# Adding P1 into a PSUM bank in a Strassen product of a graph attention kernel

## The chip, the cores and the metric

The kernel runs on one core of one Trainium2 chip. The metric is the device time of one execution in microseconds (us). Before the change it is 2387.96 us, the median of three runs (2386.17 to 2392.22). The engines are TensorE (PE in the profile; PEld is its weight load), VectorE (DVE), ScalarE (ACT), GpSimd (POOL) and SyncE (SP), which issues most of the loads. TensorE writes its results into PSUM[...]; the other memory on the core is SBUF.

## The reference

All data are fp32. The input x is 128 graphs of 64 nodes with 512 features; one adjacency matrix serves all of them.

```python
h = jnp.maximum(_layernorm(x, axis=-1), 0.0)
x = x + _L0_gnn_ref(h, adj, W_heads, ...)

def _gat_heads(x, adj, W, a):
    Wh = jnp.einsum('bnf,hfo->bhno', x, W)
    f1 = jnp.einsum('bhno,ho->bhn', Wh, a[:, :O])
    f2 = jnp.einsum('bhno,ho->bhn', Wh, a[:, O:])
    e = f1[:, :, :, None] + f2[:, :, None, :]
    e = jnp.where(e > 0, e, LEAKY_ALPHA * e)
    e = jnp.where(adj[None, None] > 0, e, NEG_INF)
    attn = jax.nn.softmax(e, axis=-1)
    return jnp.einsum('bhnm,bhmo->bhno', attn, Wh)
...
h = jax.nn.elu(_gat_heads(enc_inputs, adj, W_heads, a_heads))
h = jnp.transpose(h, (0, 2, 1, 3)).reshape(B, N, -1)
out = _gat_heads(h, adj, W_out[None], a_out[None])[:, 0]
out = jax.nn.elu(out)
ffn = jnp.maximum(out @ w1 + b1, 0.0) @ w2 + b2
y = ffn + out
...
return (y - mu) / jnp.sqrt(var + LN_EPS) * ln_gamma + ln_beta
```

There are four heads of 512 x 512 (W_heads), an output layer of 2048 x 512 (W_out) and a feed-forward of two 512 x 512 matrices (w1, w2).

## The kernel before

The 8192 rows are cut into 64 tiles of 128 rows, and four tiles make a group; 16 groups (0 to 15) are worked off one after the other. All large products are done as Strassen products in Winograd's form: a 512 x 512 by 512 x 512 product is cut into quadrants, seven products P1 to P7 of half the size are made, and the four quadrants of the result are sums of them:

- C11 = P1 + P2
- C12 = P1 + P6 + P5 + P3
- C21 = P1 + P6 + P7 + P4
- C22 = P1 + P6 + P7 + P5

The sums that the right-hand sides need are made beforehand: for the weights once, at the start (`weight_sums`, L199), and for the data in each unit (`sums`, L328).

One such product is a *unit* (`unit`, L257). A unit owns three PSUM banks: bank 1 collects P1 and P2, bank 5 collects P5 and P3, bank 6 collects P6, P7 and P4, all by TensorE's own accumulation. What the accumulation can't share between banks is done by the function `after(p)` (L263), which is called behind the last matmul of each product: it copies P1 to SBUF (s1, by ScalarE), adds t = P6 + P1 and s15 = P5 + P1 (VectorE, PSUM to SBUF), and hands each quadrant to the unit's `post`, as one bank and at most one SBUF tile to be added to it. A product may begin in a bank only when all earlier readers of that bank are done: P2 waits for the copy s1, P7 for t, P3 for s15, P4 for the addition of C22.

Four kinds of unit exist, told apart in the profile by the letter in the names (g_a is a bank of unit a, t_a its tile t):

- a (`project1`, L557): one head of one group, so 64 of them. Its `post` runs elu on each quadrant: two ScalarE operations (L541, L542) and one on VectorE (L543). C21 is then also added to C22 by GpSimd (L580), as a sum for unit b.
- b (`project2`, L599): the output layer of one group, with P1 to P7 each in four parts, one for each head. Its `post` writes the quadrants to wh, and some of its products release GpSimd to make the next sums (L610).
- c and d (`feed_forward`, L685): the two feed-forward products. `post1` of c adds the bias and takes the maximum with zero on ScalarE (L722); `post2` of d adds each part of a quadrant to the output tile o as soon as it is there, on VectorE for those straight from PSUM and on GpSimd for the tiles s1, t and s15 (L733).

The order of the products is written out: in unit a 1, 6, 5, 2, 7, 3, 4, where the late P4 of a head is put behind P1 and P6 of the next head (`late`, L593). Between two parts of a unit, small steps of other stages are strung in (`run`, L248): during the four heads of group g the scores, softmax and second attention of group g-1 (`stage_e`), and during unit b of group g the attention of group g+1, the units c and d of group g-1, the final normalisation of group g-1 (`finish`, L735) and the start of group g+2 (`stage_a`).

Each engine works off its instructions in one fixed order. That order comes from the program with priorities: what `after` issues is drawn 150 places forward (`tc.high_priority(AHEAD)`, L289). An instruction that waits holds up all behind it on its engine. The PSUM pool has six banks that go round among the units and the attention (`bank`, L78) and two for small things (`aux`).

Of the kernel before, what the change touches and what calls it, by code (L numbers as in the profile page):

```python
# [11 lines left out]
ALU = mybir.AluOpType  # L12
# [10 lines left out]
def gat_preln_kernel(  # L23
# [28 lines left out]
    nc = tc.nc  # L52
# [25 lines left out]
    def bank(name):  # L78
        return ps.tile([P, 2, T], FP, tag="mm", name=name)
# [164 lines left out]
    def flush_late():  # L244
        while late:
            late.pop(0)()
# [10 lines left out]
    def unit(name, product, post, order):  # L257


        own = {1: 1, 2: 1, 5: 5, 3: 5, 6: 6, 7: 6, 4: 6}  # L260
        gb, sb = {}, {}

        def after(p):  # L263
            if p in (1, 5, 6):
                nm = {1: "s1", 5: "s15", 6: "t"}[p]
                sb[nm] = wk.tile([P, 2, T], FP, tag=nm, name=f"{nm}_{name}")
                if p == 1:
                    nc.scalar.copy(sb[nm], gb[1])  # L268
                else:
                    nc.vector.tensor_tensor(sb[nm], gb[p], sb["s1"], ALU.add)  # L270
                post(nm, sb[nm])
            elif p == 2:
                post("c11", gb[1], None)
            elif p == 7:
                post("c22", gb[6], sb["s15"])
            elif p == 3:
                post("c12", gb[5], sb["t"])
            else:
                post("c21", gb[6], sb["s1"])

        def part(p, i, n):
            def fn():
                if i == 0:
                    subs[p] = product(p)
                    if p == own[p]:
                        gb[p] = bank(f"g{p}_{name}")
                subs[p][i](gb[own[p]], p == own[p] and i == 0)
                if i == n - 1:
                    with tc.high_priority(AHEAD):  # L289
                        after(p)  # L290
            return fn

        subs = {}
        n = product(None)
        return [part(p, i, n) for p in order for i in range(n)]
# [242 lines left out]
    def elu(dst, src, name):  # L538

        ex = wk.tile([P, 512], FP, tag="elu", name=f"ex{name}", bufs=3)  # L540
        nc.scalar.activation(ex, src, AF.Relu, scale=-1.0)  # L541
        nc.scalar.activation(ex, ex, AF.Exp, scale=-1.0)  # L542
        nc.vector.scalar_tensor_tensor(dst, ex, -1.0, src, ALU.add, ALU.max)  # L543

    def flat(ap):
        return ap.rearrange("p a b -> p (a b)")

    def quadrant(what):
        return int(what[1]) - 1, int(what[2]) - 1
# [7 lines left out]
    def project1(g, h):  # L557


        z = ZB[g]  # L560
        first = (g, h) == (0, 0)
        if h == 0:
            for b in ("11", "12", "S1", "22"):
                tag = "hS" if b == "S1" else "h" + b
                H1[b] = big.tile([P, H, 2, T], FP, tag=tag, name=f"h{b}_{g}")
        sums = {6: 0, 7: 1, 3: 2}
        blk = {1: "11", 2: "12", 4: "22", 5: "S1"}

        def post(what, a, b=None):
            if what[0] != "c":  # L570
                return
            nm = {"c11": "11", "c12": "12", "c21": "S1", "c22": "22"}[what]
            dst = H1[nm][:, h]
            if b is None:
                elu(flat(dst), flat(a), f"{what}_{g}_{h}")
            else:
                nc.vector.tensor_tensor(dst, a, b, ALU.add)  # L577
                elu(flat(dst), flat(dst), f"{what}_{g}_{h}")
            if what == "c21":
                nc.gpsimd.tensor_tensor(dst, dst, H1["22"][:, h], ALU.add)  # L580

        s = unit(
            f"a{g}_{h}", product_t(h, lambda p: ZSUM[h][sums[p]] if p in sums else z[blk[p]][:, h]),
            post, (1, 2, 6, 5, 7, 3, 4) if first else (1, 6, 5, 2, 7, 3, 4),
        )

        def next_sums():
            if h + 1 < H:
                z_sums(g, h + 1)

        return [
            s[0], lambda: (s[1](), flush_late()), lambda: (s[2](), next_sums()), s[3], s[4],
            lambda: (s[5](), late.append(s[6])),  # L593
        ]
# [4 lines left out]
    def project2(g):  # L599
        slot = {1: "11", 2: "12", 3: "12", 4: "22", 5: "S1", 6: "11", 7: "S1"}  # L600
        h1 = dict(H1)
        wh = big.tile([P, G, FO], FP, tag="wh2", name=f"wh2_{g}")
        WH2[g] = wh

        def post(what, a, b=None):
            behind = {"s1": ("11", "S1", "11"), "s15": ("S1", "22", "11"), "c11": ("12", "12", "11")}
            if what in behind:
                dst, x0, x1 = (h1[n] for n in behind[what])
                for h in range(H):
                    nc.gpsimd.tensor_tensor(dst[:, h], x0[:, h], x1[:, h], ALU.subtract)  # L610
            if what[0] != "c":
                return
            r, c = quadrant(what)
            dst = wh[:, 2 * r:2 * r + 2, c * Q:(c + 1) * Q]
            if b is None:
                nc.scalar.copy(dst, a)
            else:
                nc.vector.tensor_tensor(dst, a, b, ALU.add)

        ms = [H + h for h in range(H)]  # L620
        return unit(
            f"b{g}", product_n(ms, lambda p, i: h1[slot[p]][:, i]), post, (1, 5, 6, 2, 7, 3, 4)
        )
# [61 lines left out]
    def feed_forward(g):  # L685

        o = OUT[g]
        OT, RT = [], []

        def transpose_out(j):  # L690
            if j % 2 == 0:
                OT.append(big.tile([P, KC, T], FP, tag=f"ot{j // 2}", name=f"ot{j // 2}_{g}"))
            pt = aux([P, KC, P], f"pto{g}_{j}")
            for k in range(KC):
                nc.tensor.transpose(pt[:, k, :], o[:, j, ts(k, P)], ident)  # L695
            nc.scalar.copy(OT[j // 2][:, :, ts(j % 2, P)], pt)
            nc.gpsimd.tensor_tensor(o[:, j], o[:, j], b2s, ALU.add)
            if j == G - 1:
                bl[1] = blocks(OT, f"o{g}")

        def blocks(tt, name):
            s2, s3, s4 = new_sums(name)
            a11, a12 = tt[0][:, 0:2], tt[0][:, 2:4]
            s1, a22 = tt[1][:, 0:2], tt[1][:, 2:4]
            nc.vector.tensor_tensor(s1, s1, a22, ALU.add)
            sums(nc.vector, s1, a11, a12, a22, s2, s3, s4)
            return {1: a11, 2: a12, 3: s4, 4: a22, 5: s1, 6: s2, 7: s3}

        bl = {}

        def post1(what, a, b=None):
            if what[0] != "c":
                return
            if not RT:
                RT.extend(big.tile([P, KC, T], FP, tag=f"rt{i}", name=f"rt{i}_{g}") for i in range(2))
            r, c = quadrant(what)
            dst = RT[r][:, 2 * c:2 * c + 2]
            if b is not None:
                nc.vector.tensor_tensor(dst, a, b, ALU.add)
                a = dst  # L720
            for k in range(2):
                nc.scalar.activation(  # L722
                    dst[:, k], a[:, k], AF.Relu, bias=b1s[:, 2 * c + k:2 * c + k + 1]
                )
            if what == "c21":
                bl[2] = blocks(RT, f"r{g}")

        def post2(what, a, b=None):

            r, c = {"t": (0, 1), "s15": (1, 1), "s1": (1, 0)}.get(what) or quadrant(what)  # L730
            dst = o[:, 2 * r:2 * r + 2, c * Q:(c + 1) * Q]
            eng = nc.vector if what[0] == "c" else nc.gpsimd
            eng.tensor_tensor(dst, a, dst, ALU.add)  # L733

        def finish(j):  # L735
            t = G * g + j
            xr = load(t, "xr")
            nc.gpsimd.tensor_tensor(xr, xr, bs, ALU.add)
            y = o[:, j]
            mean, rstd = norm_stats(y, "n2", t)  # L740
            nc.vector.scalar_tensor_tensor(y, y, mean, gs, ALU.subtract, ALU.mult)
            nc.vector.scalar_tensor_tensor(y, y, rstd, xr, ALU.mult, ALU.add)
            nc.sync.dma_start(out=of[ts(t, P), :], in_=y)

        f1 = unit(f"c{g}", product_t(M1, lambda p: bl[1][p]), post1, (1, 2, 6, 5, 7, 3, 4))
        f2 = unit(f"d{g}", product_n([M2], lambda p, i: bl[2][p]), post2, (1, 6, 5, 2, 3, 7, 4))
        return (
            [lambda j=j: transpose_out(j) for j in range(G)], f1 + f2,
            [lambda j=j: finish(j) for j in range(G)],
        )  # L750
# [125 lines left out]
```

## Time and profile before

| what | us |
|---|---|
| time, median of 3 runs | 2387.96 |
| profiled span | 2389.7 |
| TensorE busy | 2324.9 |
| VectorE busy | 1455.6 |
| GpSimd busy | 1064.1 |
| ScalarE busy | 780.7 |
| one group in the steady part (1641.4 to 1784.9) | 143.5 |
| the same for the second and third group | 146.5 |

The operations that the change touches, with the mean duration of one:

| operation | engine and line | count | ns |
|---|---|---|---|
| copy of P1 to SBUF (s_a) | ACT L268 | 64 | 575 |
| t = P6 + P1 (t_a) | DVE L270 | 64 | 685 |
| s15 = P5 + P1 (s_a) | DVE L270 | 64 | 683 |
| C21 of unit a | DVE L577 | 64 | 687 |
| last step of elu, source in PSUM (C11) | DVE L543 | 64 | 682 |
| the same, source in SBUF (C12, C22) | DVE L543 | 128 | 794 |
| the same, source in SBUF (C21) | DVE L543 | 64 | 953 |
| copy of a quadrant of unit b | ACT L616 | 16 | 586 |

Lines of the profile are read like this: the start, the duration, the engine, the line of the program, the operation, and "out<-in" by the names of the tiles. A bracket at the end tells how long the engine stood idle ahead of it and what ended that. A matmul of 128x256 takes about 380 ns from its start to its end, but in a row they start every 0.216 us, so one product of a unit (eight such rows) takes 1.73 us of TensorE. A profile numbers a wait by the instruction that waited and the one that released it; "issue" stands for time in which nothing that the profile shows was awaited.

### The profile page before, as it was taken

What the parts mean: (1) busy time and instruction counts of PE and PEld (TensorE: products, weight loads), DVE (VectorE), ACT (ScalarE), POOL (GpSimd) and SP (SyncE); (2) the same over time, 40 slices, a digit from 0 to 9 for tenths busy, and PEclk for the clock granted to TensorE, in tenths of its full rate; (3) what the DMA queues carried; (4) which work ended last, traced back from release to release, by engine and by line L of the source; (5) the groups of instructions that cost most, each with busy time, mean ns of one, the idle gap of its engine ahead of it and who ended that gap; (6) DMA issues with size and microseconds to landing.
All of it is one profiled execution on the core that took longest, in us unless ns stands there. A gap on an engine that the chain in (4) does not pass through costs nothing.

```text
span 2389.7 us, 32881 instructions
## 1 busy us (share of the span) xinstructions
PE 2324.9 (97%) x11805; PEld 1943.2 (81%) x11805; DVE 1455.6 (61%) x2418; ACT 780.7 (33%) x1383; POOL 1064.1 (45%) x933
## 2 busy tenths in 40 slices
PE   6989999999999999999999999999999999999997
PEld 4768888888888888888888888888888888888885
DVE  7726475574855748476574855748466573844637
ACT  2423315133151432415234151432415233241411
POOL 5861443434444263443534444263443535533334
PEclk7999999999999999999999999999999999999999
DMA  8554454454544545454454544545454453534442
GB/s 304 190 174 139 129 171 133 137 167 131 169 130 148 164 132 178 131 161 145 137 175 128 176 128 147 167 131 181 129 162 145 139 173 130 178 119 159 160 149 93
DMA packets 257808, 366.89 MB, mean 154 GB/s; under 512 B 22216, under 2 KB 145128, under 8 KB 257648
## 3 DMA queue, kind: packets, MB, share of 16 engines
q1 hardware_dynamic: 251024, 343.82, 45.1%
q0 software_dynamic: 4512, 16.78, 1.9%
q10 hardware_dynamic: 2112, 4.19, 0.5%
q8 instruction: 95, 1.56, 0.3%
q14 instruction: 65, 0.53, 0.1%
HBM read 337.45 MB, written 27.26 MB: 153 GB/s over the span
## 4 chain that ended last, share of the span: by engine, by line
PE 93%; POOL 2%; DVE 1%; issue 1%; DMA 1%; ACT 0%; DVEq 0%; POOLq 0%; ACTq 0%
PE g_b L319 33%; PE g_a L304 31%; PE g_c L304 8%; PE g_d L319 8%; PE pz L519 4%; PE pa L668 2%; PE pzS L519 1%; PE pto L695 1%; PE pth L368 1%; PE s1pt L469 1%; PE pf L378 1%; PE s1pe L403 1%; DMA pw<-in_L_gnn_w_dram 1%; POOL pt L219 0%; POOL pt L218 0%
## 5 line engine op out<-in xcount | busy, mean ns | idle before, releaser
L319 PE MATMUL g_b<-w,h 128*128 128x256 f32 x2560 | 601.4, 381 | 0.0
L319 PEld LDWEIGHTS g_b<-w,h 128*128 128x128 f32 x2560 | 477.8, 190 | 74.6 <-issue 14.0
L304 PE MATMUL g_a<-zs_z,w 128*128 128x256 f32 x1504 | 354.6, 384 | 18.2 <-issue 15.5
L304 PE MATMUL g_a<-z,w 128*128 128x256 f32 x1520 | 359.9, 380 | 0.7 <-ACT s_a L268 0.4
L304 PEld LDWEIGHTS g_a<-zs_z,w 128*128 128x128 f32 x1504 | 287.9, 192 | 70.3 <-issue 27.8
L304 PEld LDWEIGHTS g_a<-z,w 128*128 128x128 f32 x1520 | 288.2, 190 | 54.2 <-issue 14.5
L319 PE MATMUL g_b<-w,hS 128*128 128x256 f32 x1024 | 248.2, 389 | 3.8 <-DVE z L531 3.8
L580 POOL TENSOR_TENSOR hS<-hS,h 128x512 f32<-128x512 f32 x64 | 82.1, 1282 | 369.6 <-DVE hS L543 368.9
L319 PEld LDWEIGHTS g_b<-w,hS 128*128 128x128 f32 x1024 | 190.6, 192 | 47.9 <-issue 15.3
L610 POOL TENSOR_TENSOR h<-h,h 128x512 f32<-128x512 f32 x64 | 86.9, 1358 | 226.9 <-PE g_b L319 226.9
L542 ACT ACTIVATE exc<-exc 128x512 f32<-128x512 f32 x256 | 160.6, 627 | 6.1
L543 DVE SCALAR_TENSOR_TENSOR h<-exc,h 128x512 f32<-128x512 f32 x128 | 101.6, 794 | 63.0 <-ACT exc L542 62.9
L541 ACT ACTIVATE exc<-h 128x512 f32<-128x512 f32 x128 | 80.5, 629 | 180.3 <-DVE h L577 180.3
L610 POOL TENSOR_TENSOR h<-hS,h 128x512 f32<-128x512 f32 x64 | 81.8, 1278 | 125.0 <-PE g_b L319 125.0
L330 POOL TENSOR_TENSOR zs_z<-z,zs_z 128x512 f32<-128x512 f32 x63 | 87.6, 1390 | 84.5 <-PE g_d L319 73.7
L331 POOL TENSOR_TENSOR zs_z<-z,zs_z 128x512 f32<-128x512 f32 x63 | 88.9, 1412 | 81.3 <-PE g_a L304 81.3
L329 POOL TENSOR_TENSOR zs_z<-zS,z 128x512 f32<-128x512 f32 x63 | 88.5, 1406 | 80.4 <-PE g_a L304 59.2
L319 PE MATMUL g_d<-w,rt 128*128 128x256 f32 x512 | 121.2, 379 | 1.8 <-DVE o L733 1.0
L304 PE MATMUL g_c<-ot,w 128*128 128x256 f32 x512 | 121.1, 379 | 0.7 <-ACT s_c L268 0.7
L304 PE MATMUL g_a<-zS,w 128*128 128x256 f32 x496 | 117.2, 379 | 0.0
L634 DVE SCALAR_TENSOR_TENSOR jf<-wh,ao 128x512 f32<-128x512 f32 x128 | 110.7, 885 | 0.7
L519 PE MATMUL pz<-at,hn 64*128 64x256 f32 x768 | 107.5, 403 | 3.3 <-DVE z L531 3.3
(163 smaller groups left out, 3666.8 us busy)
## 6 DMA issues: line engine op xcount, KB each, us to landing
w<-tc SPq DMA_DIRECT2D x632, 256.0 KB, 2.7
w<-in_L_gnn_W_heads_dram SPq DMA_DIRECT2D x192, 256.0 KB, 2.8
w<-in_L_gnn_W_out_dram SPq DMA_DIRECT2D x192, 256.0 KB, 2.7
w<-in_L_gnn_w_dram SPq DMA_DIRECT2D x96, 256.0 KB, 2.7
x<-in_x_dram SPq DMA_DIRECT2D x66, 256.0 KB, 2.7
xr<-in_x_dram SPq DMA_DIRECT2D x64, 256.0 KB, 2.9
out_dram<-o SPq DMA_DIRECT2D x64, 256.0 KB, 2.2
tc<-pt POOLq DMA_DIRECT2D x20, 512.0 KB, 4.4
```

The lines of the kernel that those rows point to most:

```text
L304: nc.tensor.matmul(bk[:, o, :], w[:, k, ts(o, P)], a[:, k, :], start=start and o == 0 and k == 0, stop=k == 1, skip_group_check=True,)
L319: nc.tensor.matmul(bk[:, j, :], a[:, k, ts(j, P)], w[:, k, :], start=start and k == 0 and j == 0, stop=i == len(ms) - 1 and k == 1, skip_g ...
L329: eng.tensor_tensor(s2, s1, a11, ALU.subtract)
L330: eng.tensor_tensor(s4, a12, s2, ALU.subtract)
L331: eng.tensor_tensor(s3, a22, s2, ALU.subtract)
L519: nc.tensor.matmul(banks[b][:, c, :].rearrange("p (h n) -> p h n", h=H), src[rows, off + c * P:off + (c + 1) * P], at[rows, b], start=True ...
L541: nc.scalar.activation(ex, src, AF.Relu, scale=-1.0)
L542: nc.scalar.activation(ex, ex, AF.Exp, scale=-1.0)
L543: nc.vector.scalar_tensor_tensor(dst, ex, -1.0, src, ALU.add, ALU.max)
L580: nc.gpsimd.tensor_tensor(dst, dst, H1["22"][:, h], ALU.add)
L610: nc.gpsimd.tensor_tensor(dst[:, h], x0[:, h], x1[:, h], ALU.subtract)
L634: nc.vector.scalar_tensor_tensor(junk, WH2[g][:, j], 1.0, ao[:, c, :], ALU.mult, ALU.mult, accum_out=f[:, c, j:j + 1],)
```

## The change

The change moves the addition of P1 ahead of the accumulation. Behind P6, VectorE adds s1 into bank 6 itself (PSUM plus SBUF, back to PSUM). P7 and P4 then accumulate on top of P1 + P6, so that bank 6 holds all of C21 at the end and C21 needs no addition. ScalarE copies bank 6 to SBUF as t behind that addition. P5 is copied to SBUF as it is (s5, by ScalarE) instead of being added to P1. C22 is still bank 6 plus a tile, but the tile is P5, and C12 is bank 5 plus t. In unit a both sums are written back into PSUM (C22 into bank 1, which C11 has left, C12 into bank 5), so that all steps of elu read PSUM for all four quadrants. In unit d, s1 is no longer added to the output by itself, since P1 comes with bank 6.

It is for VectorE's benefit: two additions fewer in a unit of kind a, b or c, one fewer in d, and no elu step with two inputs in SBUF. ScalarE has two copies more in a unit (three in b), and P7 now waits for VectorE's addition and ScalarE's copy.

```diff
         def after(p):
             if p in (1, 5, 6):
-                nm = {1: "s1", 5: "s15", 6: "t"}[p]
+                nm = {1: "s1", 5: "s5", 6: "t"}[p]
                 sb[nm] = wk.tile([P, 2, T], FP, tag=nm, name=f"{nm}_{name}")
-                if p == 1:
-                    nc.scalar.copy(sb[nm], gb[1])
-                else:
-                    nc.vector.tensor_tensor(sb[nm], gb[p], sb["s1"], ALU.add)
+                if p == 6:
+
+                    nc.vector.tensor_tensor(gb[6], gb[6], sb["s1"], ALU.add)
+                nc.scalar.copy(sb[nm], gb[p])
                 post(nm, sb[nm])
             elif p == 2:
-                post("c11", gb[1], None)
+                post("c11", gb[1])
             elif p == 7:
-                post("c22", gb[6], sb["s15"])
+                post("c22", gb[6], sb["s5"], gb[1])
             elif p == 3:
-                post("c12", gb[5], sb["t"])
+                post("c12", gb[5], sb["t"], gb[5])
             else:
-                post("c21", gb[6], sb["s1"])
+                post("c21", gb[6])
...
-            if b is None:
-                elu(flat(dst), flat(a), f"{what}_{g}_{h}")
-            else:
-                nc.vector.tensor_tensor(dst, a, b, ALU.add)
-                elu(flat(dst), flat(dst), f"{what}_{g}_{h}")
+            if b is not None:
+                nc.vector.tensor_tensor(to, a, b, ALU.add)
+                a = to
+            elu(flat(dst), flat(a), f"{what}_{g}_{h}")
...
-        def post2(what, a, b=None):
-
-            r, c = {"t": (0, 1), "s15": (1, 1), "s1": (1, 0)}.get(what) or quadrant(what)
+        def post2(what, a, b=None, to=None):
+
+            if what == "s1":
+                return
+            r, c = {"t": (0, 1), "s5": (1, 1)}.get(what) or quadrant(what)
```

In `project2` the name s15 becomes s5, and the copy of C21 falls to ScalarE by the branch that was there for C11.

More of the change, by code (lines that the diff above doesn't have):

```diff
@@ L567, in project1, with post @@
         blk = {1: "11", 2: "12", 4: "22", 5: "S1"}
-        def post(what, a, b=None):
+        def post(what, a, b=None, to=None):
             if what[0] != "c":
@@ L603, in project2, with post @@
         WH2[g] = wh
-        def post(what, a, b=None):
-            behind = {"s1": ("11", "S1", "11"), "s15": ("S1", "22", "11"), "c11": ("12", "12", "11")}
+        def post(what, a, b=None, to=None):
+            behind = {"s1": ("11", "S1", "11"), "s5": ("S1", "22", "11"), "c11": ("12", "12", "11")}
             if what in behind:
@@ L709, in feed_forward, with post1 @@
         bl = {}
-        def post1(what, a, b=None):
+        def post1(what, a, b=None, to=None):
             if what[0] != "c":
```

## The prediction

> **What bounds the kernel now.** I read the busy shares first, then the chain of waits, then TensorE's waits, then the timeline around the one wait that returns in every group.
>
> ```profile
> PE 2324.9 (97%) x11805; PEld 1943.2 (81%) x11805; DVE 1455.6 (61%) x2418; ACT 780.7 (33%) x1383; POOL 1064.1 (45%) x933
> PE 93%; POOL 2%; DVE 1%; issue 1%; DMA 1%; ACT 0%; DVEq 0%; POOLq 0%; ACTq 0%
> ```
>
> TensorE is busy for 97% of the span and carries 93% of the chain that ended last. VectorE, which the change relieves, is not on it, so work taken from VectorE pays only where TensorE waits for VectorE. The list of TensorE's waits shows where that is.
>
> ```profile
> PE g_a L304 <- issue: 15.7, 15, 2.1
> PE g_a L304 <- DVE s_a L270: 2.7, 1, 2.7
> PE g_c L304 <- DVE t_c L270: 2.4, 1, 2.4
> ```
>
> The columns are total, times, longest. "issue" names no engine, so I looked at one of those 15 waits in the timelines of TensorE and VectorE (start, duration, instruction).
>
> ```profile
> 1647.72 0.59 PE L304 MATMUL g_a<-z,w 128*128 128x256 f32 x2
> 1649.11 1.10 PE L304 MATMUL g_a<-zs_z,w 128*128 128x256 f32 x4 [0.79 <-issue]
> ```
>
> ```profile
> 1644.24 0.75 DVE L742 SCALAR_TENSOR_TENSOR o<-o,n2rs,xr 128x512 f32<-128x512 f32 x1 [0.44 <-POOL n2rs L346]
> 1644.91 0.68 DVE L618 TENSOR_TENSOR wh<-g_b,s_b 128x512 f32<-128x512 f32 x1
> 1645.62 1.14 DVE L634 SCALAR_TENSOR_TENSOR jf<-wh,ao 128x512 f32<-128x512 f32 x1
> ...
> 1648.32 0.69 DVE L270 TENSOR_TENSOR t_a<-g_a,s_a 128x512 f32<-128x512 f32 x1
> ```
>
> P7 of head 0 starts 0.10 us after the addition t = P6 + s1 ends (1649.01). It has to: P7 adds into the bank that t reads. P6 itself ended near 1644.87; the addition came 3.45 us later because VectorE was working off its list from the end of the previous group. The same holds in each of groups 1 to 15. The waits are 2.12 us three times (groups 1 to 3), then 0.80, 0.79, 1.35, 0.80, 0.99, 0.80, 0.80, 0.79, 0.80, 1.12, 0.64, 0.21. A table by stretches shows what the long ones cost besides (stretch; length, busy time of each engine, TensorE's granted clock, DMA share, GB/s):
>
> ```profile
> 495.70:499.20 3.50, 3.46 (x9) 2.85 (x10) 2.19 (x7) 0.00 (x0) 0.00 (x1) 0.57 0.90 322
> 787.30:790.90 3.60, 3.48 (x16) 3.13 (x17) 3.02 (x8) 0.61 (x1) 1.37 (x1) 1.00 0.84 298
> 1074.90:1078.40 3.50, 3.44 (x16) 3.09 (x17) 2.50 (x5) 0.00 (x0) 1.27 (x1) 1.00 0.95 332
> ```
>
> After 2.12 us idle (first row) the clock is 0.57 and only 9 matmuls fit; after 0.80 and 1.35 us it stays 1.00 and 16 fit. P7 and P3 together take 5.38 instead of 3.69 us, so a long wait costs 1.69 us more. These waits, 16.3 us with 5.1 us of slow clock, are all that a change at this place can win or double in the steady part.
>
> [...] the last step of elu takes 682 ns with its source in PSUM, 794 and 953 ns with it in SBUF, and the 1.14 us above overlaps a GpSimd addition begun at 1644.95. [...] No row of before writes PSUM from VectorE. [...] Here 2.12 us was enough and 1.45 us (in the tail) was not; the trace decides.
>
> **The change part by part.** *Work moved.* VectorE loses 208 additions (P1+P5 in 112 units, C21 in the 96 units of a, b and c) of some 0.685 us: 142 us, and 32 us more where elu reads PSUM: 128 x (794-682) + 64 x (953-682) ns. ScalarE gains 240 copies of 0.586 us, 141 us, and goes to about 38% of the span. GpSimd loses 16 additions (s1 into the output). Beside TensorE's 97% none of this is time by itself.
>
> *Head 0 of a group, the step that decides.* Before: t ends, P7 starts. Now: t is written into bank 6, ScalarE copies it, P7 starts. ScalarE is idle there (its line-up is s1, t, P5, with nothing waiting between). In this trace a ScalarE operation starts 0.03 us after the VectorE result it waits for (1655.96 after 1655.93), and the copy takes 0.59: +0.62 us. I take 0.69 us for the addition into PSUM, as for one into SBUF; the bounds are 0.67 and 0.80. Against this one addition leaves the list ahead of t: wh (C21 of unit b), which goes to ScalarE. From the last o before it to t the rest of the list is unchanged. Its place is 0.71 us long (1644.91 to 1645.62). In groups 1 to 3, where the next two operations run undisturbed, all of it is won: 0.62 - 0.71 = -0.09 us. In the other twelve, the two jf operations move forward into GpSimd's 1.27 us addition, and wait for it: between 0 and 0.27 us is won, so +0.35 to +0.62; I take +0.40. Sum: 12 x 0.40 - 3 x 0.09 = +4.5 us. Bounds: 15 x -0.09 = -1.4 and 15 x 0.62 = +9.3. Behind the waiting P7 stand P3 and all the next head; nothing makes the time good. The waits become about 1.2 us, short of the 2.12 that halved the clock; one or two may come to 1.7.
>
> *Heads 1 to 3.* There two more products and the late P4 lie between P6 and P7. In head 1 of the group above t ends at 1659.75 and P7 starts at 1661.71: 1.96 us for a copy of 0.62. P1+P5 ended at 1663.00, P3 started at 1663.44; now a copy of P5 on ScalarE, behind s1, t and two steps of elu (4 x 0.6), ends near 1662.4. No new wait: 0.
>
> *Units b, c, d.* t_c ends at 1587.08, P7 of c starts at 1593.90; t_b 1591.34 against 1607.20; t_d 1618.84 against 1630.02. Products of another unit lie between. 0.
>
> *Banks held longer.* elu reads bank 6 three times where one addition freed it. At the end of a group it was free at 1695.82, now near 1697.4 (P4 ends at 1695.1, then 0.6 + 0.63 + 0.69 and the hand-overs); the next use of those banks is at 1700.13. Bank 1 is held until C22 is through elu, some 7 us before its next use. 0.
>
> *Start and end.* In group 0 the wait of 2.7 us at 102 for P1+P5 goes, since that copy now runs on ScalarE. But TensorE waits again at 138 (an input load) and at 145 (a chain of GpSimd sums and loads), so it counts for little. GpSimd's chain gains about 1 us: its R waited for U on VectorE (79.67), behind an elu step that GpSimd held up for 3.01 us and that now reads PSUM. I take -1.5, between 0 and -3. In the last round P7 of c waits +0.62 more, while rt = P1 + C21 no longer passes VectorE (0.6 to 0.7 us, on the path twice): -0.5, between -1.2 and +0.6.
>
> Sum: 2387.96 + 4.5 - 1.5 - 0.5 = 2390.5; I say 2390.
>
> **Rivals.** *A: the relief wins.* VectorE arrives so much earlier that the waits of head 0 mostly go and the three slow-clock stretches with them: three long groups become like the others, -3 x 3.0 = -9, and some 3 us elsewhere: 2376. For it: 0.7 us leaves just that list, and the long waits exceed the short by 1.3 us only. Against: the copy puts 0.62 us back, and the list starts from a product of TensorE (o from d's P3, at 1628.56), so it cannot start earlier. *B: the copy wins, and the clock goes with it.* Each wait grows by 0.62 us (+9.3), and six more of them pass the unknown border between 1.45 and 2.12 us (+10): slower, 2406. For it: waits of 1.35 and 1.12 us are near. Against: most are 0.80. *C: a bank held too long* makes the first products of each group wait 1 us: +16, 2404. The 2.7 us above speak against it. *D: three parts cancel*, the forecast.
>
> **How the numbers follow.** Forecast 0.57, A 0.17, B 0.20, C 0.06. The sum of the low ends is 2388 - 1.4 - 3 - 1.2 = 2382, of the high ends 2388 + 9.3 + 0.6 = 2398. A long wait more or less makes 3 us, about what the three runs of before differ by (2386.17 to 2392.22), and the range takes in part of A and B: 2379 to 2402. Faster means below 2380.8, slower above 2395.1: A gives 0.18 with a rest of the forecast; B and C nearly all of theirs gives 0.25; between, 0.57.
>
> **What would show it.** After: P7 of head 0 starting 0.1 us after a ScalarE copy of t, which starts at once when VectorE's addition into g_a ends; waits there of 1.1 to 1.3 us in most groups; clock 1.00 behind them but for a few; no wait at 102; VectorE near 1280 us, ScalarE near 915. Wrong would make it: an addition into PSUM much above 0.7 us, that copy queued behind another ScalarE operation, a new wait of TensorE in heads 1 to 3 or at the first pz of a group, or a clock of 0.57 in most groups.

## The result, and the profile after

The changed kernel takes 2396.24 us (median of 6 runs, 2394.28 to 2398.69); the kernel before took 2385.46 us beside it (6 runs, 2383.89 to 2392.22). The ratio is 1.0040, with a 95% interval of 1.0027 to 1.0054: slower by 6 to 13 us. The prediction had said 2390, in a range of 2379 to 2402.

The page of the changed kernel, busy shares and chain:

```profile
PE 2324.6 (97%) x11805; PEld 1941.5 (81%) x11805; DVE 1297.1 (54%) x2210; ACT 902.2 (38%) x1623; POOL 1030.2 (43%) x917
PE 84%; DVE 8%; DMA 3%; POOL 2%; issue 2%; ACT 1%; SPq 0%; DVEq 0%; POOLq 0%; ACTq 0%
```

VectorE lost 158 us of work (1455.6 to 1297.1), ScalarE took over 121, and TensorE is as busy as before. But VectorE's share of the chain that ended last rose from 1% to 8%: less work, and more of it on the path. TensorE's waits say where (total, times, longest):

```profile
PE g_a L304 <- ACT t_a L270: 23.1, 14, 3.2
PE g_a L304 <- DVE g_a L575: 4.3, 3, 3.0
PE g_c L304 <- ACT t_c L270: 3.0, 1, 3.0
```

The first line stands in the place of the "issue" line of before. Of the 15 waits of that line one, of 0.25 us, was at the start; the other 14 were P7 of head 0 in groups 2 to 15 and sum to 15.45 us. The prediction said 15 groups and 16.3 us: its list has one 0.80 too many, and its "groups 1 to 3" are 2 to 4. The sum is now 23.1 us. By groups, 2 to 4 together wait 1.25 us less than before, 5 to 14 6.0 us more, and group 15 2.9 us more. The timeline around the same P7 as in the prediction (start, duration, instruction) shows how:

```profile
1643.94 0.75 DVE L743 SCALAR_TENSOR_TENSOR o<-o,n2rs,xr 128x512 f32<-128x512 f32 x1 [0.44 <-POOL n2rs L346]
...
1644.45 1.37 POOL L329 TENSOR_TENSOR zs_z<-zS,z 128x512 f32<-128x512 f32 x1 [0.54 <-PE g_a L304]
1644.61 1.76 DVE L633 SCALAR_TENSOR_TENSOR jf<-wh,ao 128x512 f32<-128x512 f32 x1
...
1647.92 0.70 DVE L269 TENSOR_TENSOR g_a<-g_a,s_a 128x512 f32<-128x512 f32 x1
1648.71 0.59 ACT L270 COPY t_a<-g_a 128x512 f32<-128x512 f32 x1 [5.45 <-DVE g_a L269]
...
1649.35 0.48 PE L304 MATMUL g_a<-zs_z,w 128*128 128x256 f32 x1 [1.53 <-ACT t_a L270]
```

Two things are to be seen. From the start of VectorE's addition to P7 it is now 1.43 us (1649.35 - 1647.92); it was 0.79 (1649.11 - 1648.32). The 0.64 us more are ScalarE's copy and its hand-over (the time from the end of one engine's operation to the start of the next that waits for it). And the list ahead of the addition did not get shorter. C21 of unit b (wh) is gone from it, but jf moved into its place, right onto GpSimd's addition, and took 1.76 us where it had taken 1.14. From the end of the last o operation to the start of the addition it was 3.33 us before (1644.99 to 1648.32) and is 3.23 now (1644.69 to 1647.92).

The two profiled spans differ by 7.1 us (2396.8 - 2389.7). With the slots of P7 of head 0 as marks this is: 2.1 us won up to group 2 (TensorE free at 345.06, before at 347.12), 7.7 us lost to longer waits there, 0.1 won on the product pairs behind them, 1.9 lost in five groups whose stretch between two such waits is 139.3 to 139.6 us instead of 139.0, and 0.35 won at the end.

### The profile page after: what moved, and what is told of

The parts are those of the page before. It is cut to its first block, busy times and chain, and to the rows that moved or that the text cites. A ratio compares the mean times of both kernels' runs of the same rounds, so it can differ in the third digit from the quotient of the medians.

```text
span 2396.8 us, 32990 instructions
## 1 busy us (share of the span) xinstructions
PE 2324.6 (97%) x11805; PEld 1941.5 (81%) x11805; DVE 1297.1 (54%) x2210; ACT 902.2 (38%) x1623; POOL 1030.2 (43%) x917
## 4 chain that ended last, share of the span: by engine, by line
PE 84%; DVE 8%; DMA 3%; POOL 2%; issue 2%; ACT 1%; SPq 0%; DVEq 0%; POOLq 0%; ACTq 0%
PE g_b L319 30%; PE g_a L304 27%; PE g_c L304 8%; PE g_d L319 6%; PE pz L519 4%; PE pa L667 2%; DVE jf L633 2%; DVE o L743 2%; PE pzS L519 1%; PE pto L694 1%; PE pth L368 1%; DMA xr<-in_x_dram 1%; DMA x<-in_x_dram 1%; DVE n2st L340 1%; PE s1pt L469 1%
## 5 line engine op out<-in xcount | busy, mean ns | idle before, releaser
L304 PE MATMUL g_a<-zs_z,w 128*128 128x256 f32 x1504 | 353.9, 384 | 23.5 <-ACT t_a L270 23.1
L541 ACT ACTIVATE exc<-g_a 128x512 f32<-128x512 f32 x256 | 152.2, 595 | 201.4 <-DVE g_a L575 172.4
L543 DVE SCALAR_TENSOR_TENSOR h<-exc,g_a 128x512 f32<-128x512 f32 x192 | 131.8, 686 | 147.0 <-ACT exc L542 147.0
L329 POOL TENSOR_TENSOR zs_z<-zS,z 128x512 f32<-128x512 f32 x63 | 83.6, 1328 | 131.2 <-PE g_d L319 70.1
L633 DVE SCALAR_TENSOR_TENSOR jf<-wh,ao 128x512 f32<-128x512 f32 x128 | 120.0, 958 | 12.2 <-ACT wh L615 12.0
L471 ACT COPY at<-s1pt 128x512 f32<-128x512 f32 x64 | 34.8, 589 | 211.4 <-PE s1pt L469 211.4
```

The source lines that it names most:

```text
L304: nc.tensor.matmul(bk[:, o, :], w[:, k, ts(o, P)], a[:, k, :], start=start and o == 0 and k == 0, stop=k == 1, skip_group_check=True,)
L329: eng.tensor_tensor(s2, s1, a11, ALU.subtract)
L633: nc.vector.scalar_tensor_tensor(junk, WH2[g][:, j], 1.0, ao[:, c, :], ALU.mult, ALU.mult, accum_out=f[:, c, j:j + 1],)
```

## The experiments

Times are medians; a ratio is to the kernel before, run on the same chip beside it. The changed kernel did not run again beside the experiments, so they are set against it by their ratios. Sums of waits come from one profiled execution each. Numbers follow the labels; there is no kernel 11.

### 1. Head 0 as before

`old` is true for head 0 of units a from group 1 on.

```
-                nc.scalar.copy(sb[nm], gb[p])
+                if old and p != 1:
+                    nc.vector.tensor_tensor(sb[nm], gb[p], sb["s1"], ALU.add)
...
+            elif old:
+                post("c21", gb[6], sb["s1"], gb[6])
```

> The changed kernel, but head 0 of units a from group 1 on as before the change: VectorE writes t and P1+P5 straight to SBUF, P7 waits for no ScalarE copy, C21 is added again. Theory 1 (the copy of t on ScalarE is the loss: the profile has VectorE's addition, then 0.09 us, then a 0.59 us copy, P7 at 1.43 us after the start of the addition, where it was 0.79): TensorE's 14 waits at head 0 fall by 0.64 us each from a sum of 23.1 to some 14 us, the time by 9 us, from 2396 to 2387. Rival (the loss lies in banks held longer, GpSimd contention or late loads, outside this path): waits stay near 23 or the time falls by less than 3 us, to 2393 or more.

Measured: 2388.69 us, ratio 1.000 (0.999 to 1.0009); the changed kernel had 1.0040. The waits at head 0:

```profile
PE g_a L308 <- issue: 13.4, 14, 1.8
```

One of the 14, of 0.25 us, is the one at the start; the other 13 are at head 0 and sum to 13.2 us. So the waits fell by 10.0 us, 0.71 a group (0.67 without group 15, whose wait is taken up below), as theory 1 said (0.64). This one path carries the loss. It is also rival A without the copy: t straight to SBUF, and b's C21 gone from VectorE. That alone doesn't beat the kernel before.

### 2. Units a alone

Units b, c and d went back to `nc.vector.tensor_tensor(sb[nm], gb[p], sb["s1"], ALU.add)`, with C21 of b and c added by VectorE again; units a stayed changed.

> Only units a as after the change; units b, c and d as before (their t and P1+P5 by VectorE, C21 of b added by VectorE again). Theory 1: the loss is that of head 0, which is in units a, so the time is that of the changed kernel within 3 us, 2393 to 2399, and head 0's waits sum to 23 within 3. Rival (taking C21 of b from VectorE's list was worth its 0.71 us a group): the waits grow by 0.7 us each to a sum of 33, time 2406.

Measured: 2398.49 us, ratio 1.0043 (1.003 to 1.0055), waits of head 0 24.5 us. Three of the four kinds of unit may change or not; the time stays. In units b, c and d the edit cost and brought nothing that can be measured: the two intervals leave room for some 4 us either way.

### 3. C21 of unit b copied by VectorE

```
-                nc.scalar.copy(dst, a)
+                eng = nc.vector.tensor_copy if what == "c21" else nc.scalar.copy
+                eng(dst, a)
```

> The changed kernel, but C21 of unit b is copied out of PSUM by VectorE instead of ScalarE, so that an operation of some 0.6 us stands again on VectorE's list ahead of t. Theory 1 (that place was worth nothing, since the next operation moved forward into GpSimd's 1.3 us addition and took 1.76 us in place of 1.14): waits of head 0 and time unchanged within 0.2 us a group, 2394 to 2399. Rival, which the prediction's best case used (the place was won): +0.6 us a group, +8 us, 2404.

Measured: 2402.15 us, ratio 1.0058 (1.0045 to 1.0071); waits of head 0 26.3 us in 14, 0.22 us a group more than the changed kernel. So the place is worth about a third of its 0.71 us, between the two theories; the time alone doesn't decide, since the intervals of the two ratios overlap. It is not a third everywhere. From the end of the last o operation to the addition it is 3.23 to 3.24 us in ten groups of kernel 3 and 3.22 to 3.23 in ten of the changed kernel: there the place is worth nothing. VectorE's timeline of the group shown above:

```profile
1644.65 0.68 DVE L616 COPY wh<-g_b 128x512 f32<-128x512 f32 x1
1645.36 1.04 DVE L634 SCALAR_TENSOR_TENSOR jf<-wh,ao 128x512 f32<-128x512 f32 x1
...
1647.96 0.70 DVE L269 TENSOR_TENSOR g_a<-g_a,s_a 128x512 f32<-128x512 f32 x1
```

One operation more, and the addition starts at 1647.96 against 1647.92. While wh is copied out of PSUM, GpSimd works on its addition (1644.36 to 1645.86) and most of it is over when jf comes: 1.04 us instead of 1.76. Beside the addition the copy out of PSUM took 0.68 us, jf 1.04, and 1.76 in the changed kernel; clear of it jf took 0.68.

### 4. The copy of t twice

```
+                if p == 6 and name[0] == "a" and name[-2:] == "_0" and name != "a0_0":
+                    nc.scalar.copy(sb[nm], gb[p])
                 nc.scalar.copy(sb[nm], gb[p])
```

> The changed kernel with ScalarE's copy of t made twice in head 0 from group 1 on. Theory 1: each of the 14 waits grows by one ScalarE interval, 0.48 us (two copies started 0.48 us apart), +6.7 us, to 2403; where waits of 1.5 to 2.1 us become 2.0 to 2.6, some matmuls behind them run at the low clock, 1.7 us a time, 2403 to 2415. Rival (P7 at head 0 does not set the time): less than 3 us more.

Measured: 2420.33 us, ratio 1.013 (1.0116 to 1.0144): 24 us more than the changed kernel by the medians, about 21 by the ratios, above the expectation. The waits at head 0 rose to 32.4 us (13 in the line below and one of 1.27 put down to GpSimd), 9.3 more instead of 6.7. Behind 11 of the 14 the clock was low (0.56 in the 3.60 us from 1376.20), where the changed kernel had two: 9 x 1.7 = 15 us. The mean granted clock of the profiled run is 0.987, of the changed kernel's 0.995.

```profile
PE g_a L306 <- issue: 31.2, 13, 3.8
```

### 5 and 6. P3 ahead of P7, in both kernels

If P7 waits, another product could stand ahead of it. The same edit, which also puts P5 ahead of P6, was made in the changed kernel (5) and in the kernel before (6):

```
-            post, (1, 2, 6, 5, 7, 3, 4) if first else (1, 6, 5, 2, 7, 3, 4),
+            post, (1, 2, 6, 5, 7, 3, 4) if first else (1, 5, 6, 2, 3, 7, 4) if h == 0 else (1, 6, 5, 2, 7, 3, 4),
```

> The changed kernel with head 0 of units a (from group 1 on) in the order P1, P5, P6, P2, P3, P7, P4: P5's copy stands before t on ScalarE, and P3, 1.73 us long, stands ahead of P7 on TensorE. Theory 1 (after the change the wait for t at head 0 is what VectorE's list and the copy cost, and nothing else loses time there): the wait of 1.65 us on average is covered, 14 x 1.5 us and the low clock behind two waits go, 2370 to 2376. Rival (the time is lost elsewhere, or P3 waits in P7's place): above 2388.

> The kernel before, in the same order of head 0. There P1+P5 is VectorE's, on the same list as t and now ahead of it, so P3 waits for that list as P7 did. Theory 1: waits of head 0 keep their length within 0.3 us, time 2384 to 2390, no gain. Rival (the order alone makes the gain, whichever engine frees P5): 2370 to 2378.

Measured: 2404.41 us, ratio 1.0052 (1.0033 to 1.0071), for 5, and 2401.00, ratio 1.0037 (1.0024 to 1.0049), for 6. Both fell outside theory 1: slower. TensorE's waits in kernel 5:

```profile
PE g_a L304 <- DVE g_a L575: 27.2, 14, 2.7
PE g_a L304 <- ACT t_a L270: 1.3, 2, 1.1
```

The wait for t is gone in all groups but one (1.10 us). In its place P4 of head 0, the third product after P7, waits for VectorE to have read C22 from bank 6; from the timeline of one group:

```profile
640.16 1.44 DVE L642 TENSOR_TENSOR s2dg<-eye,f 128x256 f32<-128x256 f32 x1
641.52 0.69 DVE L575 TENSOR_TENSOR g_a<-g_a,s_a 128x512 f32<-128x512 f32 x1
```

P4 starts at 642.26, 2.29 us late, when that addition has ended. It stands at the end of the same list: jf twice, an elu step, C12, s2dg. My theory that nothing else loses time at the start of a group was wrong. VectorE is late there, and the first product that needs it pays. But it isn't late from work alone. Ahead of the jf operations of that list stands a statistic of x, and VectorE stood idle until the input load of x had landed:

```profile
635.67 0.69 DVE L340 BATCH_NORM_STATS2 n1st<-x 128x6 f32<-128x512 f32 x1 [2.72 <-DMA x<-in_x_dram]
```

In each of the 12 groups in which P4 waits (0.84 to 2.29 us), VectorE had stood idle so for 2.1 to 3.9 us a few us earlier. No run has the load earlier or the statistic elsewhere, so what that is worth is not shown. In kernel 6 the lateness is paid in two places: 16.9 us in 13 waits of P3 for P1+P5, and 5.0 us in 7 waits for C22. The profile puts four of the 13 down to a GpSimd sum, but in all 13 P3 starts 0.10 us after VectorE's P1+P5 has ended, as t and P7 did before.

### 7 and 8. The scores two steps later

```
-            gap + score + [lambda: spread2(g)] + gap * 2 + [lambda: softmax2(g)] + gap * 5
+            gap * 3 + score + [lambda: spread2(g)] + [lambda: softmax2(g)] + gap * 5
```

> The changed kernel with the score steps two steps later, so that the two operations jf no longer stand ahead of t on VectorE; the order of TensorE is kept. Theory 1 (t is late because of that list): the list is 2.4 us shorter, the waits of head 0 go from 1.65 us to at most 0.4 on average, 2372 to 2380. Rival (t waits for something else, an input load or GpSimd): above 2390.

> The kernel before with the same score steps two steps later. Theory 1: the list ahead of t is 1.8 us shorter, all waits of head 0 of 2.1 us or less nearly go and with them the low clock, 15 and up to 5 us: 2366 to 2374, and then it is the faster of the two kernels still, by what ScalarE's copy leaves of a wait. Rival: above 2382.

Measured: 2465.59 us, ratio 1.0305 (1.0283 to 1.0327), for 7 and 2434.03, ratio 1.0179 (1.0156 to 1.0203), for 8: far slower. I had taken the two gaps out between spread2 and softmax2, and there they were needed. TensorE's waits, kernel 7 first, then kernel 8:

```profile
PE s2pe L651 <- DVE s2dg L642: 56.4, 15, 4.3
```

```profile
PE s2pe L652 <- DVE s2dg L643: 34.5, 15, 3.7
```

No wait for t is left in either. Again the list was paid for at another product. Why s2pe waits longer in 7 than in 8 is open.

### 9 and 10. The whole chain two steps later

```
-            gap + score + [lambda: spread2(g)] + gap * 2 + [lambda: softmax2(g)] + gap * 5
-            + [lambda: transpose_weights2(g)] + gap * 2 + attend[0:2] + gap + attend[2:4] + gap * 3
+            gap * 3 + score + [lambda: spread2(g)] + gap * 2 + [lambda: softmax2(g)] + gap * 5
+            + [lambda: transpose_weights2(g)] + gap * 2 + attend[0:2] + gap + attend[2:4] + gap
```

> The changed kernel with the whole chain from scores to attention of the previous group two steps later, the distances between its steps kept (with the scores alone two steps later, TensorE waited 4.33 us in most groups for s2dg). Theory 1 (VectorE's list is what the waits hang on, and the next two products, 3.46 us, can cover it): no wait at head 0 (-23 us, and -4.5 of low clock), about 0.9 us left a group at s2pe (+12): about 2381, 2374 to 2388. Rival (VectorE's backlog at the start of a group is paid at whichever product needs it first, wherever it stands): a new wait of 1.5 us or more a group, 2394 or more.

> The kernel before with the same chain two steps later. Theory 1: the waits of head 0 (15.5 us) and the low clock behind three of them (5 us) go, waits of 0.6 us for P1+P5 come in 12 groups (+8), s2pe waits no more: about 2376, 2370 to 2382. Rival (the backlog is paid elsewhere): 2386 or more.

Measured: 2382.78 us, ratio 0.9969 (0.996 to 0.9978), for 9 and 2378.22, ratio 0.9959 (0.9944 to 0.9974), for 10. Theory 1 held for both times, though not for the waits left: those for s2pe that it expected in 9 did not come, and in 10 there are 7 for P1+P5 in the steady part (4.5 us) instead of 12 (8 us). With the same edit the changed kernel stays the slower one by the medians (4.6 us; some runs of the two overlap), and the waits say why. TensorE's largest wait in the steady part of 9:

```profile
PE g_a L304 <- ACT s_a L270: 10.8, 12, 1.0
```

and around one of them, from the timeline of all engines:

```profile
358.08 0.69 DVE L575 TENSOR_TENSOR g_a<-g_a,t_a 128x512 f32<-128x512 f32 x1
...
358.80 0.60 ACT L541 ACTIVATE exc<-g_a 128x512 f32<-128x512 f32 x1 [1.63 <-DVE g_a L575]
...
359.97 0.57 ACT L270 COPY s_a<-g_a 128x512 f32<-128x512 f32 x1
...
360.59 0.48 PE L304 MATMUL g_a<-z,w 128*128 128x256 f32 x1 [0.94 <-ACT s_a L270]
```

P2 of head 1 waits for the copy of P1. P1 had long ended, but on ScalarE that copy stands behind elu of C12, and elu waits for VectorE's addition of C12, itself behind the jf operations. ScalarE stood idle for 1.63 us ahead of elu and took up the copy only behind it, at 359.97: VectorE's lateness reaches TensorE through ScalarE's list. Here too VectorE had stood idle for a load of x, for 2.8 to 4.4 us some 11 us ahead of each of the 12 waits. In 10 and 12 the waits for P1+P5 in the steady part come right behind such a load (2.8 to 3.6 us idle).

### 12 and 13. Both edits together

Kernel 12 is kernel 1 with the edit of 9; kernel 13 moves the chain one step only.

> The changed kernel with head 0 of units a as before the change (t and P1+P5 written by VectorE) and the chain of the previous group two steps later: both edits that each gave time back. Theory 1: the waits are those of the kernel before with the same later chain (6 us), without the 0.94 us that P2 of head 1 waited in 12 groups for ScalarE, and the start keeps the change's 2 to 3 us: 2376, 2370 to 2380, below both. Rival (the rest of the change costs time of its own in heads 1 to 3): 2381 or more.

> The same, with the chain one step later only, so that one first statistic of x, which waits for an input load, stands ahead of t again. Theory 1: the wait at head 0 comes back in part, 0.2 to 0.5 us a group, but waits for P1+P5 and for s1 in head 1 go: 2372 to 2382. Rival (the load sets t): waits at head 0 of 1 us, 2386 or more.

Measured: 2376.63 us, ratio 0.9955 (0.9941 to 0.9968), for 12: below both kernels, and not to be told from 10. Its waits in units a:

```profile
PE g_a L308 <- ACT s_a L272: 4.4, 5, 0.9
PE g_a L308 <- DVE s_a L268: 3.5, 6, 0.8
PE g_a L308 <- DVE g_a L579: 3.1, 4, 1.8
```

The wait for ScalarE's copy of P1 went from 12 groups to 5, not to none. Kernel 13 took 2392.85 us, ratio 1.0019 (1.001 to 1.0028), and fell outside theory 1; the time is the rival's, but not by its mechanism: waits of head 0 were 0.45 to 0.58 us in the four groups that have one, but others, mostly of 0.5 us and up to two a group, came for additions of VectorE (11.4 us in 21 waits of the steady part). A group takes 144.7 us on average in 13 and 143.5 in 12 (groups 1 to 13). The listed waits of units a in the steady part make 4.6 us of the 16 between them (13.4 against 8.8); the rest is open.

## Why the prediction was right or wrong

The time lies in the range, and the mechanism was right: head 0 decides, ScalarE's copy stands on the path, the rest cancels. The likeliest case, no change beyond 0.3%, was wrong by a little: it is 0.4%, on the side of rival B, whose losses of clock did not come. The forecast's sum was 2.5 us above before; the two profiles differ by 7.1 and the runs by 6 to 13. Of the 4.6 us between sum and profile, 3.2 are the waits of head 0 (+7.7 instead of +4.5, most of the difference in the last group) and 1.9 the five longer groups; the start gave back 0.6 more than forecast.

*Added on the path.* Predicted +0.62 us and 0.69 for the addition into PSUM. Measured +0.64 and 0.695 (mean of 64; the same addition into SBUF 0.685 before). The copy starts 0.09 us after the addition, not 0.03, and P7 0.05 after the copy. Experiment 1 takes it all away and gets 0.71 us a group back. Right.

*The place of wh.* Predicted 0.71 us won in three groups and about 0.22 in the others. From the end of the last o to the addition it was 3.23 to 3.51 us in groups 5 to 13 before, 3.36 on average, and is 3.22 to 3.23 in ten groups after: 0.13 won, by the mechanism named, since jf moves into GpSimd's addition. Right in kind, smaller in size.

*Groups 2 to 4.* Here the step failed. I took their waits of 2.12 us for a property of these groups ("the next two operations run undisturbed") and put -0.09 us there. The two operations ran undisturbed (0.69 us each in group 4) because the last o itself had met GpSimd's addition, begun at 636.75. It had taken 1.76 to 1.86 us in these groups, and 0.75 in groups 5 to 13; the first line is group 4 before. In the changed kernel this meeting came in groups 5 and 6 instead; the second line is group 5 after:

```profile
636.71 1.86 DVE L742 SCALAR_TENSOR_TENSOR o<-o,n2rs,xr 128x512 f32<-128x512 f32 x1 [0.44 <-POOL n2rs L346]
776.77 1.75 DVE L743 SCALAR_TENSOR_TENSOR o<-o,n2rs,xr 128x512 f32<-128x512 f32 x1 [0.44 <-POOL n2rs L346]
```

Where o takes the meeting, wh's whole place is won (2.88 us from o to the addition before, 2.16 after). In groups 2 to 4 after, o takes 0.75 us and jf takes the meeting. So these waits became 1.44, 1.70 and 1.97 us, 0.42 less each, not 0.09; those of groups 5 to 14 grew by 0.60 each, not 0.40. In experiments 1 to 4 too this meeting came in group 5, in 6 or in both, never in 2 to 4. That the forecast's +4.5 us is near the +4.8 of groups 2 to 14 is luck: errors of both signs in the groups, and a count of 15 for 14.

*The last group.* Its wait went from 0.21 to 3.15 us, with the low clock behind it. Nothing in the prediction covers that. GpSimd waited there for a load of xr:

```profile
2212.42 1.26 POOL L739 TENSOR_TENSOR xr<-xr,bs 128x512 f32<-128x512 f32 x1 [9.05 <-DMA xr<-in_x_dram]
```

It was issued at 2206.10 and used 6.3 us later; before, 2204.43 and 4.3 us. The longest landing of such a load was 6.5 us after and 5.1 before. In experiments 1 to 4 the wait of this group was 1.81, 0.62, 2.62 and 3.83 us, so I read it as the load's chance and not as the change's. That isn't shown: three of these four lie far above the 0.21 of before, and no run holds the load fixed.

*The clock.* Predicted "1.00 behind them but for a few": two stretches were low, and cost 4.5 us against the 5.1 of three before. Right, but with luck: two more waits, of 2.06 and 2.03 us, left it at 1.00, where one of 1.97 us lowered it (last section). B's six more didn't come. The copy twice (4) brought eleven: B was one more copy away.

*Heads 1 to 3, other units, banks.* Predicted 0. All 14 waits for t are at head 0, and experiment 2 shows nothing of units b, c and d that the times resolve. Not covered: one wait of 0.37 us of P4 for C22, and the rest of the 1.9 us in five groups, for which no wait above 0.2 us is listed; that part is open.

*Start and end.* Predicted -1.5 and -0.5; the profile has -2.1 and -0.35. The wait at 102 is gone, but waits of 2.98 us at 109.5 and 0.93 at 120.9 came for VectorE's additions of C22 and C12. P7 of c waits 3.04 us, 0.64 more. That the start's gain is the change's and not chance rests on few profiles: TensorE was free for P7 of group 2 between 343.7 and 346.9 in the changed kernel and experiments 1 to 4, at 347.1 in the kernel before and, for P3, at 348.3 in experiment 6.

*Busy times.* Predicted 1280 and 915 us for VectorE and ScalarE, measured 1297 and 902: jf takes 958 ns on average instead of 885, 9 us in 128.

## What to carry to other kernels

Taking work from a busy engine pays only where TensorE waits for its list, and there count what is put back on the path: here 0.1 to 0.2 us came off in most groups and 0.64 went on, 14 times. If a wait comes from an engine's list, moving the waiting product moves the wait. Thin the list at that moment, by moving other work on it to where the engine has slack (the attention chain, two steps later: about 10 us in the kernel before), and keep the distances between the steps of what is moved. Look also for what only waits in the list: here a statistic of x held it up for an input load. And an operation taken from a list can leave its time to a neighbour that then runs beside another engine's work and takes longer (here jf beside GpSimd's addition, 1.76 us instead of 1.14).

## What the runs showed of the hardware

How long TensorE may idle before its clock drops isn't one number here. In the profiles of the kernels before and after, behind the first 150 us, TensorE waited 20 times for more than 1.2 us. The 11 waits of up to 1.71 us left the granted clock at 1.00, and so did two of 2.03 and 2.06 us. With the other seven (1.97 us, three of 2.12, 2.40, 3.04 and 3.15) it went to 0.50. In the changed kernel 1.97 us did (first row), 2.06 did not (second), 3.15 did (stretch; length, busy time of each engine, granted clock, DMA share, GB/s):

```profile
635.60:639.20 3.60, 3.58 (x12) 2.92 (x13) 2.21 (x6) 1.59 (x3) 0.94 (x1) 0.69 0.70 243
782.10:785.70 3.60, 3.60 (x17) 3.19 (x18) 1.59 (x4) 1.57 (x3) 1.26 (x1) 1.00 1.02 357
2221.80:2225.40 3.60, 3.60 (x9) 2.88 (x10) 1.22 (x4) 1.56 (x3) 1.58 (x2) 0.50 0.99 326
```

These waits differ in where they fall in time. In the two profiles all changes of the granted clock lie whole steps of 3.413 us apart (17 changes before, 9 after, to within 0.005 us). With six of the seven waits the clock stayed at 0.50 for one step, 1.7 us lost, with the one of 3.15 us for two. In experiment 5 waits of the same 2.29 us, before 353.54 and before 642.26, went both ways. Here are the two steps that hold the first wait, then the step that holds the second and the one behind it:

```profile
349.37:352.79 3.42, 1.88 (x9) 1.32 (x7) 3.42 (x7) 1.20 (x2) 1.26 (x1) 1.00 0.54 184
352.79:356.20 3.41, 2.66 (x12) 2.38 (x13) 2.67 (x6) 1.78 (x5) 0.00 (x0) 1.00 0.14 46
639.51:642.92 3.41, 1.12 (x6) 0.67 (x5) 3.28 (x5) 1.87 (x4) 1.26 (x1) 1.00 0.44 147
642.92:646.33 3.41, 3.41 (x10) 2.69 (x9) 1.30 (x2) 2.46 (x5) 0.00 (x0) 0.50 0.00 0
```

The first wait lies across the border of two steps, 1.54 us in one and 0.75 in the next, and the clock stays. The second lies in one step, and the next step runs at 0.50. Cut at the steps in the same way, the 13 waits of before and after that left the clock at 1.00 have at most 1.96 us in one step (1.96 of the 2.03, 1.76 of the 2.06), and the other seven have 1.97 to 2.40. So these 20 waits part by the idle time within one step, not by their length. Why, and whether it holds for other kernels, the traces don't show. From the start of the span the changes lie 1.27 us behind whole steps before and 2.10 after, so the same wait can fall otherwise from one profile to the next: whether one of about 2 us costs 1.7 us more is in part chance.
